# Moving one running sum in an attention loop from GpSimd to VectorE

## The chip, the core and the metric

The kernel runs on one core of one Trainium2 chip. The metric is the device time of one execution in microseconds (us), lower is better; a kernel is judged by the median of several executions. A profile of one more execution shows what each engine did: TensorE (PE; its weight loads are PEld), VectorE (DVE), ScalarE (ACT), GpSimd (POOL), and SyncE (SP), whose queue here issues most of the DMA transfers.

## What is computed

A vision transformer block on a 48 x 48 map of 768 channels (2304 tokens, 12 heads of 64), followed by a Fourier layer. All data are float32. Cut to what matters here:

```python
xn = layernorm(x, ln1_g, ln1_b)
q, k, v = heads of (xn @ qkv_w + qkv_b)
attn = einsum('bqc,bkc->bqk', q * scale, k)
attn = attn + rel_h[:, :, :, :, None] + rel_w[:, :, :, None, :]   # relative positions by row, by column
attn = softmax(attn, axis=-1)
out = einsum('bqk,bkc->bqc', attn, v) @ proj_w + proj_b
x = shortcut + out
x = x + gelu(layernorm(x) @ mlp_w1 + mlp_b1) @ mlp_w2 + mlp_b2
# then: 2-D real FFT, two block-diagonal complex layers with relu and soft shrinkage, inverse FFT, + x
```

## The kernel before

The kernel goes through these stages: queries, keys and values (to about 400 us in the profile), attention (to about 1470 us), output projection, MLP, Fourier layer. Many matrix products are done by a seven-product (Strassen-like) scheme, which needs sums and differences of weight blocks.

**Attention.** Heads are taken in pairs: six pairs `pr`, and for each pair six chunks `c` of 384 queries, so 36 chunks. For a chunk, the loop over 18 tiles of 128 keys calls `scores` (L692): TensorE multiplies queries with keys (L678) and adds the relative positions by a second product (L687) into one of three score banks `sp`; ScalarE writes the exponentials (L697) into `exps`, a view of `main`; VectorE adds them up in twos into `pairs` (L871). Then the weighted sum `op` of the values is made in six parts of three key tiles (L710), and `between` (L817) hangs small jobs in front of these parts:

- part 1: `denominators` (L724) turns and adds up the exponentials on VectorE. L722 belongs to its preparation.
- part 4: `inverses` (L734): a small product on TensorE (L739) gathers the denominators; VectorE takes the reciprocal into `rden` (L741) and adds the denominators to `sums` (L742); the inverses are added to `inverse` (L743). `sums` and `inverse` are used once after attention (L1005, L1006), to see whether any denominator was out of range.
- part 5: `left_apart` (L754) writes `rden` to `den_d` in DRAM (L757); `stored` (L788) writes the result of the chunk before (L791); `spread_out` (L763) reads the inverses of the chunk before back as copies in all partitions (L770); `scaled` (L776) multiplies the weighted sum of two chunks before by its copies on VectorE (L782), and ScalarE adds a bias (L785).
- `relative` (L296) makes the position terms of a later chunk. Each call issues 24 transfers `terms` on SyncE (L317, L321). In the last chunk of a pair (`c` = 5) it is called twice, in front of parts 0 and 2, and once in front of part 3 of the chunk before.

`finish` (L748) copies `op` away on ScalarE (L751), and the next chunk's exponentials follow on the same engine.

**Pieces of weight sums.** GpSimd has a job of its own beside attention: the block sums of the MLP weights, in 48 pieces. `asked` (L796) fetches a piece (L802), `summed` (L805) does four adds of 128x192 (`left` or `right`, L164 to L167 or L175 to L178) and writes it to DRAM (L815). There is one buffer `seven` for it, so a fetch waits for the write before it. Two pieces go with each chunk: `asked` at key tile 2 and in front of part 1, `summed` at key tile 12 and after the chunk.

**What sets the order.** In attention the orders of TensorE, SyncE, ScalarE, VectorE and GpSimd are those of the program text (`manual_schedule`). Each engine runs its instructions in that order. Waits come from the data and from the buffers: `rden`, `spread` and `o` have two buffers each, by the pool's line

```python
o_pool = att.enter_context(tc.tile_pool(name="att_o", bufs=2))
```

so the reciprocal of a chunk waits until the add of L743 and the transfer of L757 of two chunks before have read their `rden`.

## Time and profile before

| what | value |
|---|---|
| median of 3 runs | 2897.19 us (2890.52 to 2905.95) |
| the profiled execution, its own time | 2883.8 us |
| its span, first to last instruction | 2882.0 us |
| mean granted TensorE clock | 0.991 |
| TensorE busy in the span | 2803.0 us, 97% |
| VectorE, ScalarE, GpSimd busy | 1722.7, 944.7, 658.6 us |
| L741 reciprocal, 24x32, 36 times | 0.346 us each (median) |
| L742 add on VectorE, 24x32, 36 times | 0.116 us each (median) |
| L743 add on GpSimd, 24x32, 36 times | 0.456 us each (median), 0.241 to 1.782 |

How to read it: busy time is the time in which an engine had an instruction under way. A line such as `DVE rden L741 <- POOL inverse L743: 56.5, 9, 12.6` in the list of waits says that VectorE's instructions of line 741, which write rden, stood idle until GpSimd's line 743 was done: 56.5 us in total, 9 times, 12.6 us at the longest. In a timeline a row gives start, duration, engine, line, operation, output and input, how many alike were merged, and in brackets the idle time of the engine in front of it with what ended it. The clock is given as a share of full speed.

### The profile page before, as it was taken

The page shows a single profiled execution, that of the slowest core. Times are in us where ns is not written, and L with a number is a line of the kernel's source. Part 1 is how long each engine was busy: PE and PEld are TensorE (multiplying, and loading weights), DVE is VectorE, ACT ScalarE, POOL GpSimd, SP SyncE. Part 2 cuts the span into 40 slices and gives each one's busy share as a digit, 9 for nine tenths or more (in the row PEclk, how much of TensorE's full clock was granted, in tenths as well). Part 3 has the DMA queues.
Part 4 walks back from the last instruction along what each step waited for, and adds up shares of the span by engine and source line. Part 5 has one row for each costly group of instructions (what it writes and reads, how often), then busy time and mean ns, then how long its engine had stood idle before and what let it go on. Part 6 is the DMA issues. An engine that isn't in the chain of part 4 may idle for free. (4 is left out here: it accounts for less than half of the span.)

```text
span 2882.0 us, 40848 instructions
## 1 busy us (share of the span) xinstructions
PE 2803.0 (97%) x15759; PEld 1720.7 (60%) x15759; DVE 1722.7 (60%) x2520; ACT 944.7 (33%) x1502; POOL 658.6 (23%) x626
## 2 busy tenths in 40 slices
PE   8999999999999899999999999999999999999998
PEld 4555656555556555565555555555555555556887
DVE  5434247667576575576666756675665556566665
ACT  1101136656566464575521210122111211012332
POOL 3505024334344343300044010011000100002432
PEclk9999999999999999999999999999999999999999
DMA  4535387585886847836352223322322322223254
GB/s 156 172 110 173 91 175 174 127 183 127 166 188 129 192 124 154 163 61 111 78 189 86 81 94 115 114 96 103 115 89 103 140 96 80 112 101 115 61 161 138
DMA packets 230715, 363.45 MB, mean 126 GB/s; under 512 B 26180, under 2 KB 203964, under 8 KB 224368
## 3 DMA queue, kind: packets, MB, share of 16 engines
q1 hardware_dynamic: 215720, 306.80, 40.4%
q0 software_dynamic: 12352, 52.11, 5.8%
q8 instruction: 127, 2.08, 0.3%
q10 hardware_dynamic: 2440, 1.84, 0.2%
q14 instruction: 76, 0.62, 0.1%
HBM read 211.59 MB, written 85.35 MB: 103 GB/s over the span
## 5 line engine op out<-in xcount | busy, mean ns | idle before, releaser
L697 ACT ACTIVATE main<-sp 128x768 f32<-128x768 f32 x648 | 520.1, 813 | 32.2 <-PE sp L687 25.7
L1320 PE MATMUL h<-shared,w 128*128 128x384 f32 x1512 | 504.1, 486 | 0.7 <-issue 0.7
L871 DVE TENSOR_TENSOR pairs<-pairs,main 128x1536 f32<-128x1536 f32 x252 | 460.6, 1828 | 32.4 <-ACT main L697 6.1
L687 PE MATMUL sp<-terms,select 64*128 64x384 f32 x1296 | 417.9, 639 | 0.0
L1320 PEld LDWEIGHTS h<-shared,w 128*128 128x128 f32 x1512 | 287.0, 190 | 202.0 <-issue 2.5
L1380 DVE TENSOR_TENSOR main<-o,main 128x384 f32<-128x384 f32 x540 | 299.2, 556 | 38.7 <-PE o L1378 0.2
L678 PE MATMUL sp<-shared 64*128 64x384 f32 x1296 | 270.4, 494 | 18.6 <-ACT main L697 17.6
L678 PE MATMUL sp<-qT,kT 64*128 64x384 f32 x1296 | 269.6, 493 | 19.3 <-ACT main L697 19.3
L1378 PE MATMUL o<-w,hs 128*128 128x384 f32 x648 | 262.5, 487 | 1.5 <-DVE hs L165 1.0
L1378 PE MATMUL o<-w,hT 128*128 128x384 f32 x648 | 245.1, 487 | 3.0 <-DVE main L1380 3.0
L1395 POOL TENSOR_TENSOR main<-main,acc 128x384 f32<-128x384 f32 x9 | 11.4, 1264 | 924.2 <-DVE main L1380 665.3
L1326 ACT ACTIVATE hT<-c,vec 128x384 f32<-128x384 f32 x108 | 66.7, 618 | 464.9 <-DVE c L1332 464.9
L710 PE MATMUL op<-main,shared 128*64 128x384 f32 x1296 | 218.3, 488 | 0.0
L710 PE MATMUL op<-main,v 128*64 128x384 f32 x1296 | 217.0, 488 | 0.0
L871 DVE TENSOR_TENSOR pairs<-main 128x1536 f32<-128x1536 f32 x36 | 64.7, 1796 | 225.8 <-ACT main L697 225.8
L1332 DVE TENSOR_TENSOR c<-h,u 128x384 f32<-128x384 f32 x108 | 60.2, 557 | 212.9 <-PE h L1320 212.9
L687 PEld LDWEIGHTS sp<-terms,select 64*128 64x128 f32 x1296 | 127.0, 190 | 87.0 <-issue 4.4
L1378 PEld LDWEIGHTS o<-w,hT 128*128 128x128 f32 x648 | 122.7, 190 | 90.2 <-DVE main L1380 5.9
L1378 PEld LDWEIGHTS o<-w,hs 128*128 128x128 f32 x648 | 122.5, 190 | 89.4 <-DVE main L1380 4.5
L537 PE MATMUL m<-main 128*128 128x384 f32 x504 | 164.2, 487 | 2.1 <-DVE main L187 1.7
L678 PEld LDWEIGHTS sp<-qT,kT 64*128 64x128 f32 x1296 | 119.4, 189 | 73.2 <-ACT main L697 24.4
L678 PEld LDWEIGHTS sp<-shared 64*128 64x128 f32 x1296 | 120.0, 190 | 71.3 <-ACT main L697 21.9
(205 smaller groups left out, 3627.4 us busy)
## 6 DMA issues: line engine op xcount, KB each, us to landing
w<-w_d SPq DMA_DIRECT2D x72, 1344.0 KB
w_d<-seven POOLq DMA_DIRECT2D x48, 672.0 KB, 5.5
terms<-col_parts SPq DMA_DIRECT2D x432, 72.0 KB
seven<-in_w_blocks_dram POOLq DMA_DIRECT2D x48, 384.0 KB, 5.0
terms<-row_hi SPq DMA_DIRECT2D x216, 72.0 KB
terms<-row_lo SPq DMA_DIRECT2D x216, 72.0 KB
main<-in_qkv_w_dram SPq DMA_DIRECT2D x36, 384.0 KB
z<-zt SPq DMA_DIRECT2D x48, 192.0 KB
```

What stands on the lines that cost most here:

```text
L537: nc.tensor.matmul(bank, a[:, c, :], b[:, c, :], start=(first and c == 0), stop=(c == 2), skip_group_check=not first,)
L678: nc.tensor.matmul(sp[:, j, :G], kT[at, ts(kt, P)], qT[at, ts(c, G)], start=first, stop=not first,)
L687: nc.tensor.matmul(sp[:, j, :G], select[at, a % 2], ready[pr, c][at, a // 2, b], start=first, stop=not first,)
L697: nc.scalar.activation(p, sp[:, :, :G], AF.Exp, scale=HD**-0.5)
L710: nc.tensor.matmul(op[ts(j, 64)], v[:, kt, ts(j, 64)], exps[:, kt, j, :], start=(kt == 0), stop=(kt == NT - 1),)
L871: nc.vector.tensor_tensor(pairs, so_far, exps[:, ds(kt - 1, 2)], ALU.add)
L1320: nc.tensor.matmul(bank[i], a[:, c, :], b[:, c, :], start=(start and c == 0), stop=(c == 2), skip_group_check=not start,)
L1326: nc.scalar.activation(h[:, i, ts(k, G)], src, AF.Gelu, bias=col(V_B1 + tiles_of_chunk(n)[i]))
L1332: nc.vector.tensor_tensor(t, src, other, ALU.add)
L1378: nc.tensor.matmul(bank[k], a, b, start=start, stop=True, skip_group_check=not start)
L1380: nc.vector.tensor_tensor(dst, bank[k], dst, ALU.add)
L1395: nc.gpsimd.tensor_tensor(x12, x12, acc[i], ALU.add)
```

## The change

The add of the inverses goes from GpSimd's queue to VectorE's, at the same place of the program text. Operands, shapes and the number of adds (36) are the same.

```diff
                     rden = o_pool.tile([ND, 32], F32, name="rden")
                     nc.vector.reciprocal(rden, den[:ND, :32])
                     nc.vector.tensor_tensor(sums[:ND], sums[:ND], den[:ND, :32], ALU.add)
-                    nc.gpsimd.tensor_tensor(inverse[:ND], inverse[:ND], rden, ALU.add)
+                    nc.vector.tensor_tensor(inverse[:ND], inverse[:ND], rden, ALU.add)
                     made[pr, c] = [rden]
```

In the order of VectorE's instructions the add now stands behind L742 and in front of L782 (in the first two chunks, which have no L782, in front of L871). On GpSimd 36 adds leave the queue, most of them from between a fetch of a piece and its adds, ten of them from the end, where they followed the last piece.

## The prediction

> **What bounds the kernel now.** I read in this order: the page's busy times, the waits between 400 and 1480 us (the attention stage, where the edited line runs), the timeline of each engine around the longest of these waits, and the windows for the granted clock. I number the 36 chunks of attention k = 6·pr + c.

> The page first:

> ```profile
> PE 2803.0 (97%) x15759; PEld 1720.7 (60%) x15759; DVE 1722.7 (60%) x2520; ACT 944.7 (33%) x1502; POOL 658.6 (23%) x626
> ```

> TensorE is busy for 97%, so an edit on VectorE and GpSimd can be worth only what it does to TensorE's idle time and to its clock. The waits show how much idle time attention holds (us in total, times, longest):

> ```profile
> POOL inverse L743 <- DVE sums L742: 231.9, 10, 29.3
> DVE rden L741 <- POOL inverse L743: 56.5, 9, 12.6
> PE sp L678 <- ACT main L697: 36.9, 11, 8.2
> DVE o L782 <- DMA spread<-den_d: 24.5, 6, 10.0
> ```

> TensorE stands still for 36.9 us because ScalarE's exponentials have not emptied the score banks. VectorE waits 56.5 us for GpSimd and 24.5 us for copies of the inverses. These two can both be the cause, so I followed one case through the engines. Chunk 19:

> ```profile
> 993.38 0.55 POOL L802 DMA_DIRECT2D seven<-in_w_blocks_dram  x1 [10.28 <-DMA w_d<-seven]
> 993.94 0.27 POOL L743 TENSOR_TENSOR inverse<-inverse,rden 24x32 f32<-24x32 f32 x1
> 994.24 0.34 DVE L741 RECIPROCAL rden<-small 24x32 f32<-24x32 f32 x1 [11.61 <-POOL inverse L743]
> 994.56 0.53 DVE L782 TENSOR_TENSOR o<-ot,spread 128x384 f32<-128x384 f32 x1
> 995.13 0.62 ACT L785 ACTIVATE o<-o,vec 128x384 f32<-128x384 f32 x1 [18.78 <-DVE o L782]
> 996.88 1.65 PE L678 MATMUL sp<-qT,kT 64*128 64x384 f32 x4 [7.05 <-ACT main L697]
> 998.64 1.48 PE L678 MATMUL sp<-qT,kT 64*128 64x384 f32 x4
> ```

> GpSimd's add for a past chunk stands in its queue behind a weight piece, which waits for the write of the piece before (10.28 us). The reciprocal takes one of two rden buffers, and the add still holds it. Behind the reciprocal stand L742 and L782 on VectorE; L785 on ScalarE waits for L782, and the next exponentials stand behind L785. The end is a gap of 7.05 us on TensorE. Of 11.61 us some 4.5 are absorbed.

> The other cause, at the end of a head pair (chunk 24):

> ```profile
> 1147.17 1.13 SPq L770 DMA_DIRECT2D spread<-den_d  x2
> ...
> 1153.54 0.34 DVE L741 RECIPROCAL rden<-small 24x32 f32<-24x32 f32 x1 [12.56 <-POOL inverse L743]
> ...
> 1156.18 1.65 PE L678 MATMUL sp<-shared 64*128 64x384 f32 x4 [8.25 <-ACT main L697]
> ```

> Here the GpSimd wait is the longest of all, but the spread copy that L782 needs was itself issued only at 1148.30 (end of the row), because SyncE first issues the 48 terms transfers of two relative() calls (1106.68 to 1146.15). Without GpSimd, VectorE would wait for this.

> **The change part by part.**
> *Removed: the add on GpSimd, and the wait of L741 for it.* In the instruction order of the changed kernel the reciprocals have lost GpSimd from their waits; the orders of TensorE, ScalarE and SyncE are the same. I matched each GpSimd wait with the TensorE gap behind it. Chunks 15 (0.83 us) and 17 (2.21): no gap. Chunk 18: 5.79 gave 2.26; 19: 11.61 gave 7.05; 20: 6.52 gave 2.20; 21: 3.48 gave 0.94; 23: 5.93 gave 1.49; 24: 12.56 gave 8.25; 25: 7.60 gave 3.24. Together 25.43 of the 36.9 us. The rest (6.30 at chunk 6, 4.02 at 12, 0.54 at 33) stands behind spread copies and stays.

> *What is late next.* After a spread copy's last issue, L782 started 2.2 to 2.6 us later where it had waited for it (chunks 6, 12, 18, 30). Chunk 18: issued by 955.81, L782 at 958.01; it waited 0.69 us for the copy even after GpSimd, so nothing is gained. Chunk 24: 1148.30 + 2.4 = 1150.7 against 1153.86, so 3.1 us are gained for 23 and 24 together (SyncE's backlog begins in chunk 23 and isn't moved by its gap). Chunk 19: issued by 978.14, so there by 980.5; the reciprocal could have run at 994.24 - 11.61 = 982.6: all gained. By the same test all of 20, 21 and 25 is gained (25: there by 1173.2, needed at 1176.9). Gaps: 7.05 + 2.20 + 0.94 + 3.1 + 3.24 = 16.5 us.

> *The clock behind a gap.* After chunk 19's gap three pairs of key tiles take 996.88 to 1001.84 = 4.96 us; after chunk 20's gap of 2.20, at full clock, 1029.64 to 1032.21 = 2.57. So 2.4 us more; likewise 1.4 us after chunk 25. The windows agree:

> ```profile
> 997.00:1001.00 4.00, 4.00 (x18) 2.50 (x18) 1.21 (x1) 2.49 (x4) 2.15 (x3) 0.50 1.05 122
> 1029.00:1033.00 4.00, 3.36 (x24) 2.30 (x26) 1.28 (x1) 3.99 (x6) 1.56 (x2) 1.00 0.92 128
> ```

> (the clock is the third figure from the end: 0.50 and 1.00). [...] The trace shows the clock down after 3.24 (chunk 25) and 2.26 us (chunk 18) too, so I take its 3.8 us: 16.5 + 3.8 = **20.3 us**. Chunk 24 keeps a gap of about 8.25 + 1.49 - 3.1 = 6.6 us and its slow restart.

> *Added: 36 adds of 24x32 on VectorE, between L742 and L782.* The nearest row is L742, the same shape with one operand in PSUM: 0.12 us; L1010 with both operands in SBUF took 0.16 us. I take 0.16, so 36 x 0.16 = 5.8 us of VectorE. Nothing of it is on TensorE's path: in most chunks ScalarE, done with L785, still waits for the weighted sum (L751, 2.36 us), and the matches above show 2.5 (chunk 21) to 4.6 us (chunk 19) of VectorE's lateness absorbed before TensorE stops; at chunks 6, 12, 18, 24 and 30 VectorE is waiting for a spread copy anyway. If that cover were gone it would cost those 5.8 us. It can't gain, being new work. [...] Cost on the path: 0, upper bound 5.8.

> *Moved: GpSimd itself.* It sheds 19.5 us of adds, most of them in the shadow of its own transfers (the add at 993.94 ran while the fetch issued at 993.38 was on its way), so its last piece still ends near 1202; the pieces are read by the MLP after 1500, some 300 us later. Its software queue issues the same transfers. The last add no longer runs between two residual adds at 1465, worth about 0.6 us to GpSimd and nothing to TensorE.

> **The sum.** The profiled execution took 2883.8 us (span 2882.0): 2883.8 - 20.3 = 2863.5. The median of the runs is 2897.19, 13.4 us above, and the fastest timed run is 2890.52, so the profiled one is a short one. From the median the same saving gives 2876.9. Where the 13.4 us lie no trace shows. From chunk 18 to 25 attention ran at GpSimd's pace, (1187.31 - 956.63) / 7 = 33.0 us a chunk, against 28.1 later ((1437.38 - 1212.96) / 8); slower transfers of GpSimd there go into the time one for one and would go away with the change. I give half of it to that: **2870 us**.

> **The rivals.**
> *More comes back (0.20).* In the timed runs GpSimd is later than in the profile, so that all 13.4 us were its doing: 2863; with the gaps and restarts of chunks 18 and 24 gone too (25.4 + 8.5 = 33.9 us) 2850. For: GpSimd's pace. Against: the spread copies of 18 and 24.
> *The spread copies take the waits over (0.15).* Chunks 19, 20 and 25 have 2 to 4 us before the copy is what is late, and another 3 that are absorbed. If SyncE's transfers come 5 us later once attention runs faster, half of the saving is lost: about 2887, which can't be told from no change. For: SyncE is 32 us behind at chunk 5 (den_d at 601.45, its reciprocal at 569.43). Against: its backlog starts anew with each chunk's own rows, which move with TensorE.
> *Slower (0.05).* With GpSimd never held, its transfers fall differently among the 48 terms transfers ahead of each head pair's end, and these grow. Place: the L770 copies of chunks 6, 12, 18 and 24. Price: 1 us of TensorE for each us. It makes up for the gain from 5.1 us each, and makes the kernel slower by over 0.5% from (20.3 + 14.5) / 4 = 8.7 us each: 2912. The 48 took 39.5 us here; the end without GpSimd's traffic (chunk 29, 1289.4 to 1325.3) took 36, so the whole of that traffic is worth 3.5 us. Hence the small chance.
> That the wait stays is excluded by the order of the instructions.

> **The numbers.** The main case has 0.60, from 2857 (all of the 13.4, and a little more) to 2882. A measurement of this kernel can tell about 0.5%, 14.5 us. Main case and first rival are faster by over that, 0.80; the second rival is within, 0.15; the last 0.05. Range 2852 to 2888.

> **What would show it.** Right: no wait of L741 for GpSimd; the L782 wait for spread copies grown from 24.5 us to about 24.5 + 6.5 (chunk 18) + 9.5 (chunk 24) - 0.7 = 40; TensorE's wait for the exponentials down from 36.9 to about 20 us, at chunks 6, 12, 18 and 24; the new add at 0.12 to 0.2 us; GpSimd's pieces ending near 1200. Wrong: L782 waiting at chunks 19, 20 or 25, TensorE idle over 30 us, or the new add over 1 us at the median.

## The result, and the profile after

The changed kernel took 2866.09 us in the median (2860.45 to 2868.14) beside 2894.8 us of the kernel before: a ratio of 0.9892, with a 95% interval of 0.986 to 0.9924. Forecast were 2870 us. In a second comparison it took 2861.75 beside 2892.48 us (0.9891, 0.9865 to 0.9916). Its profiled execution took 2860.45 us (span 2858.7), 23.35 us less than the profiled one of before.

The page's busy times of the changed kernel:

```profile
PE 2796.2 (98%) x15759; PEld 1717.6 (60%) x15759; DVE 1729.1 (60%) x2556; ACT 946.3 (33%) x1502; POOL 630.9 (22%) x590
```

VectorE has 36 instructions more and 6.4 us more work, GpSimd 36 fewer; TensorE's number is the same. The waits of the attention stage (us in total, times, longest):

```profile
PE sp L678 <- ACT main L697: 21.6, 6, 7.1
...
DVE o L782 <- DMA spread<-den_d: 41.4, 8, 10.7
...
DVE rden L741 <- PE small L739: 16.5, 30, 1.1
```

The reciprocal waits for GpSimd no more; its 56.5 us are gone from the list, and what it still waits for is the small product of its own chunk. TensorE's wait for the exponentials fell from 36.9 to 21.6 us. The wait of L782 for spread copies grew from 24.5 to 41.4 us. Chunk 19, which had the gap of 7.05 us:

```profile
986.60 0.34 DVE L741 RECIPROCAL rden<-small 24x32 f32<-24x32 f32 x1 [0.43 <-PE small L739]
986.87 0.12 DVE L742 TENSOR_TENSOR sums<-sums,small 24x32 f32<-24x32 f32 x1
986.98 0.18 DVE L743 TENSOR_TENSOR inverse<-inverse,rden 24x32 f32<-24x32 f32 x1
987.09 0.56 DVE L782 TENSOR_TENSOR o<-ot,spread 128x384 f32<-128x384 f32 x1
```

The new add puts off L782's start by 0.11 us, and TensorE has no gap behind this chunk. At chunk 24 the gap stays, and the copy is now named as what it waits for:

```profile
1137.83 0.56 DVE L782 TENSOR_TENSOR o<-ot,spread 128x384 f32<-128x384 f32 x1 [7.69 <-DMA spread<-den_d]
...
1140.16 1.65 PE L678 MATMUL sp<-shared 64*128 64x384 f32 x4 [4.07 <-ACT main L697]
```

The last reciprocal of attention starts at 1442.70 instead of 1463.85 us, so 21.15 of the span's 23.3 us were won up to there. The other 2.2 lie behind attention: from that reciprocal to the end it took 1418.16 us before and 1415.96 after. In the eight other traces used below, the last two left out, it took between 1414.9 and 1420.3 us, so these 2.2 us are no more than executions differ by.

### The profile page after: what moved, and what is told of

It reads as the page before. It is cut to its first block, busy times and chain, and to the rows that moved or that the text cites. A ratio compares the mean times of both kernels' runs of the same rounds, so it can differ in the third digit from the quotient of the medians.

```text
span 2858.7 us, 40827 instructions
## 1 busy us (share of the span) xinstructions
PE 2796.2 (98%) x15759; PEld 1717.6 (60%) x15759; DVE 1729.1 (60%) x2556; ACT 946.3 (33%) x1502; POOL 630.9 (22%) x590
## 5 line engine op out<-in xcount | busy, mean ns | idle before, releaser
L697 ACT ACTIVATE main<-sp 128x768 f32<-128x768 f32 x648 | 521.3, 812 | 31.2 <-PE sp L687 24.0
L871 DVE TENSOR_TENSOR pairs<-pairs,main 128x1536 f32<-128x1536 f32 x252 | 461.8, 1833 | 30.4 <-ACT main L697 3.8
L687 PE MATMUL sp<-terms,select 64*128 64x384 f32 x1296 | 415.4, 634 | 0.0
L678 PE MATMUL sp<-shared 64*128 64x384 f32 x1296 | 268.4, 491 | 12.7 <-ACT main L697 11.7
L678 PE MATMUL sp<-qT,kT 64*128 64x384 f32 x1296 | 267.2, 489 | 9.9 <-ACT main L697 9.9
L871 DVE TENSOR_TENSOR pairs<-main 128x1536 f32<-128x1536 f32 x36 | 64.5, 1790 | 239.9 <-ACT main L697 239.9
L687 PEld LDWEIGHTS sp<-terms,select 64*128 64x128 f32 x1296 | 126.4, 188 | 85.5 <-issue 2.4
L678 PEld LDWEIGHTS sp<-shared 64*128 64x128 f32 x1296 | 119.5, 189 | 64.4 <-ACT main L697 14.6
L678 PEld LDWEIGHTS sp<-qT,kT 64*128 64x128 f32 x1296 | 118.9, 188 | 61.7 <-ACT main L697 12.2
```

Source lines behind the costliest of these rows:

```text
L678: nc.tensor.matmul(sp[:, j, :G], kT[at, ts(kt, P)], qT[at, ts(c, G)], start=first, stop=not first,)
L687: nc.tensor.matmul(sp[:, j, :G], select[at, a % 2], ready[pr, c][at, a // 2, b], start=first, stop=not first,)
L697: nc.scalar.activation(p, sp[:, :, :G], AF.Exp, scale=HD**-0.5)
L871: nc.vector.tensor_tensor(pairs, so_far, exps[:, ds(kt - 1, 2)], ALU.add)
```

## The experiments

**Is it the wait, or the place of the add?** Two kernels take the one without the other. The first leaves the add on GpSimd and gives rden more buffers:

```diff
-                    rden = o_pool.tile([ND, 32], F32, name="rden")
+                    rden = o_pool.tile([ND, 32], F32, name="rden", bufs=8)
-                    nc.vector.tensor_tensor(inverse[:ND], inverse[:ND], rden, ALU.add)
+                    nc.gpsimd.tensor_tensor(inverse[:ND], inverse[:ND], rden, ALU.add)
```

(against the changed kernel; against the kernel before it is the first pair alone.)

> The kernel before, with eight rden buffers in place of two; the add stays on GpSimd. Theory (all that the change brought was that the reciprocal no longer waits for a buffer held by GpSimd's late add): as fast as the changed kernel, 2866 us within 5, no wait of L741 for GpSimd, TensorE's wait for the exponentials near 21 us, spread copies awaited for about 41 us. Rival (GpSimd gained by shedding 36 adds, or the place of the add matters): as slow as before, 2895 us.

2864.14 us, 0.9896 (0.9872 to 0.9921), and beside it, on the same chip, the changed kernel:

> The changed kernel itself, beside the others on the same chip: 2866 us, about 1.1% under the kernel before. It is the base for the other three.

2861.75 us, 0.9891. The two can't be told apart. The waits of the kernel with eight buffers, in which none of L741 for L743 is left:

```profile
POOL inverse L743 <- DVE sums L742: 199.2, 9, 29.3
...
DVE o L782 <- DMA spread<-den_d: 38.4, 8, 9.0
...
PE sp L678 <- ACT main L697: 17.4, 6, 5.3
```

GpSimd still makes the sum (its first row), and the picture is otherwise that of the changed kernel. So the gain is the buffer's; which engine adds is of no account. The second kernel is the changed one with the hold put back:

```diff
                     nc.vector.tensor_tensor(inverse[:ND], inverse[:ND], rden, ALU.add)
+                    nc.gpsimd.tensor_tensor(again[:ND], again[:ND], rden, ALU.add)
```

> The changed kernel, and besides it GpSimd adds the same inverses into a second accumulator that nobody reads, at the old place of its queue. Theory: the hold on rden is back, so 2895 us within 8, L741 waits for GpSimd again for 50 to 80 us in all. Rival (what counts is which engine makes the sum that is used): 2866 us.

2906.83 us, 1.0046 (1.0027 to 1.0066): the gain is lost, with 12 us more than the 2895 expected, where 8 were allowed. Its waits (lines are moved by two or three):

```profile
DVE rden L743 <- POOL again L746: 76.8, 11, 11.0
...
PE sp L680 <- ACT main L699: 48.5, 14, 7.1
```

Its reciprocal waited longer than before's (76.8 against 56.5 us), and GpSimd's last piece was issued for writing at 1218.39 instead of 1202.06. What made GpSimd later in this kernel was not taken apart.

**Is attention's pace that of GpSimd?** One more add in each of the 48 pieces, in the kernel before and in the changed one:

```diff
                         nc.gpsimd, *(seven[:, a] for a in range(4)), [seven[:, a] for a in (4, 5, 6)]
                     )
+                    nc.gpsimd.tensor_tensor(
+                        seven[:, 6], seven[:, 2 if k else 1], seven[:, 5], ALU.subtract
+                    )
```

> The kernel before with a fifth add on GpSimd in each of its 48 pieces (the last difference of the four, written once more; same result). Theory (GpSimd's pace is attention's pace): about 46 pieces x 1.5 us = 69 us later at chunk 25, and less only by what the first chunks still absorb: 2950 to 2965 us, L741's wait for GpSimd at 150 us or more. Rival (GpSimd's lateness is mostly absorbed, as at chunks 15 and 17): under 2915 us.

> The changed kernel with the same fifth add in each of GpSimd's 48 pieces. Theory (nothing waits for GpSimd any more): 2864 us within 6, GpSimd's last piece written near 1270 us instead of 1207. [...]

The kernel before went to 2933.91 us, 1.0136 (1.0104 to 1.0168): 38 us slower. The changed kernel stayed at 2864.53 us, 0.9896 (0.9865 to 0.9927). Each is the median of two executions, 16 to 17 us apart. The last write of a piece in the kernel before, without and with the fifth add:

```profile
1202.06 0.91 POOL L815 DMA_DIRECT2D w_d<-seven  x1 [0.41 <-POOL seven L178]
...
1239.01 0.91 POOL L818 DMA_DIRECT2D w_d<-seven  x1 [0.41 <-POOL seven L813]
```

The same in the changed kernel:

```profile
1206.71 0.91 POOL L815 DMA_DIRECT2D w_d<-seven  x1 [0.41 <-POOL seven L178]
...
1287.78 0.91 POOL L818 DMA_DIRECT2D w_d<-seven  x1 [0.41 <-POOL seven L813]
```

In the kernel before GpSimd ended 37 us later and the time rose by 38 (by 42 between the profiled executions). In the changed one it ended 81 us later (1287.78, where about 1270 was expected) and the time stayed. So GpSimd's lateness did go into the time about one for one, and goes there no longer. My 2950 to 2965 was too high: I gave the fifth add 1.5 us a piece and left the others as they were. But it made GpSimd 27.1 us busier in the kernel before (658.6 to 685.7) and 75.1 us in the changed one (630.9 to 706.0). The old adds did not keep their length. L178 took 1.50 us on average in the kernel before, 1.15 with the fifth add, where VectorE waited 113.2 us for GpSimd (150 or more were expected), and 1.55 in the changed kernel with it, where VectorE doesn't wait. In this order:

```profile
L178 POOL TENSOR_TENSOR seven<-seven 128x192 f32<-128x192 f32 x24 | 35.9, 1497 | 0.0
```

```profile
L178 POOL TENSOR_TENSOR seven<-seven 128x192 f32<-128x192 f32 x24 | 27.7, 1153 | 0.0
```

```profile
L178 POOL TENSOR_TENSOR seven<-seven 128x192 f32<-128x192 f32 x24 | 37.2, 1549 | 0.0
```

What the length goes with, the trace of the kernel before shows add by add: 62 of the 192 adds of pieces ran beside a VectorE TENSOR_TENSOR for less than an eighth of their time and took 0.58 to 0.60 us; 100 ran beside one for over seven eighths of it and took 1.81 us on average. That the loop regulates itself by this, a waiting VectorE letting GpSimd catch up, is my estimate from these numbers. The means by kernel do not show it: in the changed kernel without the fifth add, where VectorE doesn't wait for GpSimd either, L178 took 1.41 us.

**Are the remaining gaps the spread copies?** The scaling of L782 is moved a chunk later, so that its copy has a chunk more (this kernel is called e4 below):

```diff
-                        spread = o_pool.tile([P, G], F32, name="spread")
+                        spread = o_pool.tile([P, G], F32, name="spread", bufs=3)
...
-                        work[5] += [partial(spread_out, 0), partial(scaled, 1), stored]
+                        work[5] += [partial(spread_out, 0), partial(scaled, 2 if c == 3 else 1), stored]
                     else:
-                        work[5] += [partial(spread_out, 1), partial(scaled, 1)]
+                        work[5] += [partial(spread_out, 1), partial(scaled, 2)]
```

> The changed kernel, with L782 scaling the weighted sum of three chunks before instead of two (three spread buffers), so that each spread copy has one chunk more to arrive. Theory (all of TensorE's gaps that the change left are the spread copies at chunks 6, 12, 18, 24 and 33): gaps of 7.06 + 7.06 + 2.10 + 4.07 + 0.69 = 21.0 us go, and about 6.8 us of slow restarts behind the three longest, so 28 us less: 2838 us. Rival (behind the copies SyncE's 48 terms transfers are late themselves, or ScalarE is next): half of it, 2852 us, with new waits of L678 at the same chunks.

2855.88 us, 0.9868 (0.984 to 0.9896): some 6 of the 28 us, beside the changed kernel's 2861.75 on the same chip, so the theory failed. Gaps stood at chunks 6, 12, 18 and 24 still, and VectorE's timeline named another transfer:

```profile
607.68 0.56 DVE L782 TENSOR_TENSOR o<-ot,spread 128x384 f32<-128x384 f32 x1 [8.65 <-DMA oT<-o]
```

L782 writes one of two `o` buffers, and the store of the older one (L791) is issued on SyncE beside the copy, behind the same 48 terms transfers. The copy had hidden it. With three `o` buffers too:

```diff
-                        o = o_pool.tile([P, G], F32, name="o")
+                        o = o_pool.tile([P, G], F32, name="o", bufs=3)
```

> As e4, and with three o buffers as well (the gather matrix moved into a free piece of shared to make room): in e4 L782 no longer waited for its spread copy but for the store of an older result, oT<-o, which stands at the same place of SyncE's queue. Theory (SyncE's lateness at the pairs' ends is all that is left, and both buffers carry it): gaps of e4 of 5.03 + 2.53 + 2.05 + 3.46 = 13.1 us and some 5 us of restarts go: e4's 2856 less 18 = 2838 us, no wait of L678 for ScalarE over 1 us after chunk 0. Rival (the terms transfers themselves come late, since they stand in the same queue): TensorE waits for terms at L687, 2848 us or more.

2835.77 us (2832.98 to 2837.67), 0.9798 (0.9784 to 0.9811). That is faster than both kernels. In its list of waits ScalarE now waits for the weighted sum at all 36 chunks, that is, TensorE leads everywhere, and TensorE's wait for the exponentials is 0.6 us, at the first chunk:

```profile
ACT ot L751 <- PE op L710: 97.0, 36, 11.1
...
PE sp L678 <- ACT main L697: 0.6, 1, 0.6
```

The gaps of chunks 6, 12, 18, 24 and 33 were thus SyncE's lateness in two forms. The 48 terms transfers themselves came in time: the list has no wait of TensorE for terms.

**Would that have helped the kernel before?** The same two edits without the change:

> The kernel before (add on GpSimd, two rden buffers) with the same three spread and three o buffers and the scaling a chunk later. Theory (from about chunk 15 to 25 attention goes at GpSimd's pace, so a gap removed in front of that is waited for again there): no gain of note, 2890 us within 8, and L741 waits for GpSimd longer than the 56.5 us of before. Rival (the two kinds of stall are independent): the gaps of chunks 6, 12 and 33, 6.30 + 4.02 + 0.54, and 3 us of restarts go, 2878 us.

2886.71 us, 0.9974 (0.9956 to 0.9991): within the theory's range, though 7.5 us of gain by the ratio is not none. The waits and the longest gap:

```profile
DVE rden L741 <- POOL inverse L743: 75.8, 10, 17.4
...
PE sp L678 <- ACT main L697: 44.6, 9, 13.1
```

```profile
845.15 1.65 PE L678 MATMUL sp<-shared 64*128 64x384 f32 x4 [13.06 <-ACT main L697]
```

The gaps of chunks 6 and 12 are gone, and chunk 14, which had none, has one of 13.06 us: attention came earlier, GpSimd did not. The same edit is worth some 27 us behind the change (0.9798 against 0.9891) and 7.5 without it.

**Does work at the add's place cost anything?** Four and nine more adds of 128x384 on VectorE in front of L782:

```diff
                     nc.vector.tensor_tensor(inverse[:ND], inverse[:ND], rden, ALU.add)
+                    for _ in range(4):          # and 9
+                        nc.vector.tensor_tensor(pad, pad, pad, ALU.add)
```

The kernel with four is called e9 below.

> The changed kernel, and behind its new add, in front of L782, four more adds of 128x384 on VectorE (a pad of zeros added to itself), some 2.3 us a chunk, 36 x 2.3 = 83 us of VectorE in all. Theory (2.5 to 4.6 us of lateness on VectorE are absorbed at this place before TensorE stops, so the new add of 0.18 us costs nothing): 2866 us within 6. Rival (work at this place is on TensorE's path, so that the new add costs its 36 x 0.18 = 6 us too): 2920 us or more.

> As e9 with nine such adds, about 5.1 us a chunk, 184 us of VectorE in all. Theory: now more than is absorbed, by about 0.6 us in most chunks and 2.5 us in those with c = 3; chunks 6, 12, 18 and 24 wait for their spread copies anyway. 25 x 0.6 + 6 x 2.5 = 30 us and a few restarts: 2890 to 2910 us. Rival (some larger cover, such as the other chunks' work, absorbs it still): 2870 us.

With four: 2876.49 us, 0.9935 (0.991 to 0.996), about 11 us over the changed kernel (2866 within 6 was expected). None of it is in the chunks. The last reciprocal starts at 1441.62 us (1442.70 in the changed kernel), and the gaps are those of the spread copies and one of 0.19. The loss lies at the end of attention, where no chunk follows and the scheduler mixed the pads into the preparation of the projection: the last scaling but one of L782 started at 1449.73 instead of 1444.11 us. The projection's first product:

```profile
1452.94 13.53 PE L937 MATMUL m<-col_parts,og 128*128 128x384 f32 x34 [7.46 <-ACT ot L755]
```

In the changed kernel this wait is 0.58 us. With nine: 2940.74 us, 1.0157 (1.0129 to 1.0186), against the 2890 to 2910 expected:

```profile
PE sp L678 <- ACT main L697: 63.9, 33, 3.4
...
649.21 0.92 PE L678 MATMUL sp<-qT,kT 64*128 64x384 f32 x4 [1.50 <-ACT main L697]
```

A gap of 1.5 to 3.4 us in nearly every chunk, most often 1.50. Of about 5.1 us some 3.6 are absorbed there, 2.5 in others, not up to 4.6. The stretch behind the last reciprocal was 14 us longer besides (1430.0 against 1416.0). So the new add, at 0.18 us, is free in the chunks, by a wide margin; 2.3 us more are absorbed in all but one of them, 5 us in hardly any. At the end of attention there is no cover.

## Why the prediction was right

**The wait and the gaps behind it.** Right, and shown from both sides: eight buffers without the move give the whole gain, the move with the hold put back gives none. The gaps of chunks 19, 20, 21, 23 and 25 are gone, as the matching of waits with gaps had it.

**What is late next.** Right in kind: the wait for copies rose to 41.4 us where about 40 were forecast, and TensorE's wait fell to 21.6 where about 20 were. That the sums fit is in part luck, as the single sizes were off both ways. Chunk 18 kept 2.10 us as said. Chunk 24 kept 4.07 instead of 6.6. Chunk 12 has 7.06, where it had 4.02 and was to keep it, and chunk 6 has 7.06 instead of 6.30. The forecast gave a copy 2.2 to 2.6 us from its last issue to the start of L782; at chunks 6 and 12 of the changed kernel it took 4.87 and 5.84 us. What held these transfers is not known. From 5.29 (eight buffers) to 2.00 us (changed kernel with the fifth add) chunk 12's gap differs so much between runs that one profile can't size it. L782 also waited 0.55 us at chunk 20, which I had named as a sign against me; it was absorbed.

**The clock.** The trace bears out the 3.8 us. The mean granted clock in the 8 us behind a gap was 0.82, 0.79, 0.79, 0.68, 0.61 and 0.82 in the kernel before (chunks 6, 12, 18, 19, 24, 25), and 0.63, 0.81 and 0.67 in the changed one (6, 12, 24). What is missing to 1, times 8 us, makes 11.9 us lost before and 7.1 after. Chunks 19 and 25, for which the 3.8 stood, make 4.0 of this. So of the 21.15 us won in attention 15.3 are gaps (36.9 - 21.6) and 4.8 slow restarts. After the 2.26 us of idleness at chunk 18 of the kernel before TensorE ran at 0.50 too; the last section has the rows.

**The new add.** 0.178 us in the median where 0.16 was taken, and free. Three of its 36 runs were longer, 0.195, 0.557 and 1.095 us, each beside an add of GpSimd. In the last chunk GpSimd's residual add was under way:

```profile
1442.33 1.80 POOL L896 TENSOR_TENSOR main<-main,pb 128x768 f32<-128x768 f32 x1 [234.71 <-DVE part L730]
...
1443.08 1.09 DVE L743 TENSOR_TENSOR inverse<-inverse,rden 24x32 f32<-24x32 f32 x1
```

GpSimd's ends at 1444.13, the add at 1444.17. In the two others GpSimd's add had started first as well, and ended 0.04 to 0.05 us before VectorE's. A fourth met a GpSimd add that started after it, and took 0.178 us. What lengthened the three the trace does not name. (The longest single add of a piece in the trace of before took 2.22 us, less than the 2.5 us absorbed.)

**The sum.** 20.3 us were forecast from the profile, and 23.35 lie between the two profiled executions: gaps 15.3 (16.5 forecast), slow restarts 4.8 (3.8 forecast), 1.0 more in attention, and the 2.2 behind it by which executions differ anyway. To the 20.3 I added 6.7, half of the 13.4 us by which the profiled execution of before was shorter than the median. The medians differ by 28.7 us (30.7 in the second comparison), 5.4 to 7.4 more than the two profiled executions. That this fits is luck: the half was a guess, and each difference hangs on one profiled execution, which in the changed kernel too was the fastest of its four. The two kernels with the fifth add show that time which GpSimd loses was lost by the kernel before and is not lost by the changed one. That GpSimd was later in the timed runs than in the profiled one is not shown, as they have no trace. Their spread could fit it: 18 runs of the kernel before lie between 2885.72 and 2906.48 us, 6 of the changed one between 2857.87 and 2866.84. But the two runs of the changed kernel with the fifth add, where nothing waits for GpSimd, are 16.0 us apart as well.

**The rivals.** The copies took over no more of the wait in total than was counted. Of the slower case nothing came: the 48 terms transfers ahead of chunks 6, 12, 18 and 24 took 39.8, 37.6, 35.8 and 38.3 us, against 39.1, 36.6, 36.3 and 39.5 before, and it needed 5.1 us more in each. Its small chance rested on a misreading, though. In chunk 29 SyncE stood idle first: the 48 were issued from 1292.33 to 1325.20 and took 32.9 us, not 36, so that GpSimd's traffic could have been worth 6.6 us instead of 3.5.

## What to carry to other kernels

An engine that is 23% busy can still set the pace, if a small job of the main path stands in its queue behind a long chain of transfers and holds a buffer; look for the instruction whose wait names that engine, and follow it to the gap. More buffers are as good a cure as moving the job: here eight in place of two were; whether three would do was not tried. Then ask what the removed wait had hidden: here a copy, behind it a store, and each has to get its buffer before the next gain shows; in the other order most of that gain would have been eaten.

## What was not expected of the hardware

The length of a gap alone did not tell whether TensorE restarted slowly: it did after gaps of 2.26 us (the kernel before, chunk 18) and 2.17 us (the kernel with nine adds, at 867 us), and not after 2.20 us (the kernel before, chunk 20). In the kernel with nine adds two gaps of 2.60 us differ: behind that at 492.98 us the clock was 1.00 in the next 5 us, behind that at 996.05 it was 0.66.

```profile
957.58:960.99 3.41, 1.15 (x12) 0.54 (x8) 0.56 (x1) 2.39 (x5) 0.00 (x0) 1.00 0.86 199
960.99:964.40 3.41, 3.41 (x16) 2.03 (x12) 1.72 (x1) 2.33 (x4) 2.36 (x3) 0.50 0.71 85
...
1025.84:1029.25 3.41, 1.60 (x12) 0.75 (x8) 0.85 (x3) 1.36 (x3) 0.82 (x2) 1.00 0.74 191
1029.25:1032.66 3.41, 3.02 (x24) 2.09 (x24) 0.94 (x1) 3.40 (x6) 1.22 (x2) 1.00 0.92 122
```

The gap of 2.26 us lies whole in one stretch of the grid, and the next stretch runs at 0.50. The gap of 2.20 us is cut in two, 1.81 and 0.39, and the clock stays. In the kernel with nine adds the same grid, laid where its products became slow and fast again (867.5 and 870.9 us), cuts the two gaps of 2.60 us into about 1.6 and 1.0, and into about 0.3 and 2.3. I counted all the stretches of the grid that ran at full clock between 400 and 1500 us, 623 in the traces of the kernel before and of the changed one: where TensorE was idle for 1.88 us or less, the next one ran at 1.00, and where it was idle for 2.26 us or more (9 times), the next one ran at 0.50, without an exception. Behind attention it was not so: the next one ran at 0.50 after 0.67 us of idleness in the stretch from 2851.97 us of the kernel before, and after 1.64 us in that from 1913.40 us of the changed one.

GpSimd's adds of 128x192 took 0.58 us at the shortest and 2.22 at the longest in the kernel before, where L178's mean was 1.50 us; it was 1.15 in the kernel in which VectorE waited for GpSimd most (113.2 us).
